# A LayerNorm's shift moved to ScalarE and ahead of other work in a two-layer graph network

## The chip, the cores and the metric

The kernel runs on one core of one Trainium2 chip. Its time is the device time of one execution in microseconds, lower is better; where several executions were measured, the median is given. The profile is of one further execution of the same program.

The core has five engines that run side by side, each with a queue of its own: TensorE (PE, matrix products), VectorE (DVE), ScalarE (ACT), GpSimd (POOL), and SyncE (SP), which here only starts transfers. Each engine takes its instructions in the order in which the program lists them, and an instruction waits at the head of its queue until what it reads is there.

## The reference

There are 128 samples. Each has 128 nodes with 512 features (`x`) and a 128x128 matrix (`adj`) of zeros and ones. Two residual layers follow each other; cut to what matters:

```python
# layer 0: graph attention with 8 heads of 64 features
feats = einsum('bnf,hfu->bhnu', x, W)
dense = e_self[..., :, None] + e_neigh[..., None, :]        # scores of node i and node j
dense = leaky_relu(dense, 0.2) + NEG_BIG * (1 - adj)        # mask
att   = softmax(dense)
x     = layernorm(x + relu(att @ feats + b))                # "first LayerNorm"
# layer 1: two hypergraph convolutions
out = Dn * (H @ (Be * (H.T @ (x @ W)))) + b                 # one convolution; H = (adj != 0)
h = layer_norm(relu(conv1(x)))                              # 512 -> 1024 features
y = conv2(h)                                                # 1024 -> 512, the "second convolution"
x = layernorm(x + (y + x))
```

Everything is float32. The LayerNorms' weights and the biases come in as inputs.

## The kernel before

The kernel handles two samples (a "pair") at a time, 64 pairs. Up to five pairs are in work at once: while one pair's scores are computed, the pair before it is in the attention, the one before that in the convolutions. Every step is registered with a lag (how many rounds after its pair's start) and a time within the round, whose length in this list is 38.6:

```python
T = 38.6
...
time += (p + lag) * T
...
for _, fn, args in sorted(todo, key=lambda e: e[0]):
    fn(*args)
```

The times set nothing but the order in which the instructions stand in the engines' queues. The chip then runs as fast as the waits let it.

The attention scores of a pair lie in `nb` (128 rows, two samples, 8 heads x 128). They arrive by a transfer that spreads a row over all partitions, and pass four engines in four groups `(g, q)` (sample, half of the heads): GpSimd adds the mask, ScalarE adds the node's own score and applies the leaky ReLU, VectorE takes the negated maximum, ScalarE the exponential.

```python
def masked(p, s, g, q):                      # GpSimd, 128x512
    ...
    nc.gpsimd.tensor_tensor(t, t, neg[...], op=ALU.add)

def leaky(p, s, g, q):                       # ScalarE, four of 128x128
    ...
        nc.scalar.activation(t, t, AF.Prelu, bias=s["ft"][:, g, h, 0:1], alpha=SLOPE)

def largest(p, s, g, q):                     # VectorE, "first maximum" is that of group (0, 0)
    ...
    nc.vector.tensor_reduce(s["nm"][:, g, hs], ..., AX.XY, ALU.max, negate=True)

for (g, q), tm, (lag, tl), (lagx, tx), te, tt in (
    ((0, 0), 31.0, (1, 33.2), (1, 33.9), 2.7, 18.1), ((0, 1), 32.2, (1, 35.0), (1, 36.7), 4.6, 18.15),
    ((1, 0), 34.2, (1, 37.5), (2, 2.0), 7.8, 21.5), ((1, 1), 35.4, (2, 6.0), (2, 7.3), 7.9, 21.55),
):
    at(1, tm, masked, g, q)
    at(lag, tl, leaky, g, q)
    at(lagx, tx, largest, g, q)
    at(2, te, exponential, g, q)
    at(2, tt, e_transpose, g, q, since=1)
```

The pair before it is at its first LayerNorm in the same stretch. VectorE adds the residual and takes mean and variance (`mv`), VectorE adds epsilon, GpSimd raises to the power -1/2 (`rs`), GpSimd makes the shift, minus mean times `rs` (`sh`), and ScalarE gives the output:

```python
def residual(p, s, g):
    y = s["y"][:, g, :]
    nc.vector.scalar_tensor_tensor(y, y, 0.0, s["x"][:, g, :], op0=ALU.max, op1=ALU.add)
    moments(p, s, "a", y, g)                 # bn_stats, bn_aggr -> s["mv", "a"]

def rstds(p, s, key):
    ...
    nc.vector.tensor_scalar(ve, s["mv", key][:, :, 1], EPS, None, op0=ALU.add)
    s["rs", key] = small.tile([P, 2], F32, tag="rs", name=f"rs{key}_{p}")
    nc.gpsimd.tensor_tensor(s["rs", key], ve, mhalf, op=ALU.pow)

def first_output(p, s, g):
    t = s["y"][:, g, :]
    nc.scalar.activation(
        t, t, AF.Identity, bias=s["sh"][:, g:g + 1], scale=s["rs", "a"][:, g:g + 1]
    )

at(2, 34.5, first_output, 0)
at(2, 34.55, first_output, 1)
```

The first product of the convolutions reads this output. It is the first matmul of the next round, and ScalarE evicts it (`zT`) for the hidden products `ph`:

```python
at(3, 0.0, propagate, 0)                     # TensorE: pz = y, R
at(3, 0.9, propagate, 1)
at(3, 1.1, z_evict, 0)                       # ScalarE: zT = pz
at(3, 2.0, z_evict, 1)
chain("ph", 3, (2.0, 3.8, 5.6, 7.35, 9.1, 12.65, 14.4, 4.0, 7.5, 11.0), hidden, HALF)
```

The matrix products of a pair are done with seven block products in place of eight. They run into three PSUM banks X, Y and W in the order 1, 2, 6, 5, 7, 4, 3 (the first seven times in the list), with X copied by ScalarE after products 1, 6 and 7 (the last three times). For the second convolution (`py`) that is:

```python
chain("py", 3, (24.2, 29.4, 27.7, 32.9, 31.2, 35.35, 37.1, 26.2, 29.6, 33.1), weigh,
      QU, 1, until=LAST)
...
at(3, 31.3, y_sum, 0, 0, 0, "Y", until=LAST)
at(3, 34.9, y_sum, 1, 1, 2, "W", until=LAST)   # VectorE: third copy + bank W after product 5
at(4, 0.1, y_sum, 0, 1, 1, "W", until=LAST)    # VectorE: second copy + bank W after product 3
at(3, 37.2, y_sum, 1, 0, None, "X", until=LAST)  # ScalarE: bank X after product 4
```

Product 3 adds on to bank W, so it waits until the sum of the second line has read that bank. Between these, VectorE also evicts the propagator (`r_evict`, 35.8, which needs the transferred `dnb`) and works out the deviation of the hidden layer (`h_rstd`, 36.0). The attention's transposes (`e_transpose`, `eT`) follow on VectorE at 18.1 and 21.5, the attention's products (`attend`, `pav`) at 20.65 and 25.95 on TensorE.

Of the kernel before, what the change touches and what calls it, by code (L numbers as in the profile page):

```python
# [8 lines left out]
F32 = mybir.dt.float32  # L9
AF = mybir.ActivationFunctionType  # L10
ALU = mybir.AluOpType
# [9 lines left out]
def kernel(  # L21
# [45 lines left out]
    nc = tc.nc  # L67
    G, N, F = x.shape
    P = 128
# [15 lines left out]
    small = ctx.enter_context(tc.tile_pool(name="small", bufs=4))  # L85
# [212 lines left out]
    LAST = PAIRS - 1  # L298
    steps = []

    def step(lag, time, since=0, until=PAIRS):

        def keep(fn):
            steps.append((lag, time, fn.__name__, range(since, until), fn, ()))
            return fn
        return keep

    def at(lag, time, fn, *args, since=0, until=PAIRS):
        steps.append((lag, time, fn.__name__, range(since, until), fn, args))
# [331 lines left out]
        )  # L641

    for (g, q), tm, (lag, tl), (lagx, tx), te, tt in (
        ((0, 0), 31.0, (1, 33.2), (1, 33.9), 2.7, 18.1), ((0, 1), 32.2, (1, 35.0), (1, 36.7), 4.6, 18.15),
        ((1, 0), 34.2, (1, 37.5), (2, 2.0), 7.8, 21.5), ((1, 1), 35.4, (2, 6.0), (2, 7.3), 7.9, 21.55),
    ):
        at(1, tm, masked, g, q)
# [4 lines that stand above are left out]
# [64 lines left out]

    at(2, 26.2, residual, 0)
    at(2, 30.7, residual, 1)
    at(2, 31.5, rstds, "a")

    @step(2, 33.0)
    def first_shift(p, s):
        s["sh"] = small.tile([P, 2], F32, tag="sh", name=f"sh_{p}")
        for g in range(2):
            nc.gpsimd.tensor_scalar(
                s["sh"][:, g:g + 1], s["mv", "a"][:, g, 0:1], -1.0, s["rs", "a"][:, g:g + 1],
                op0=ALU.mult, op1=ALU.mult,
            )

    def first_output(p, s, g):  # L730
# [2 lines left out]
            t, t, AF.Identity, bias=s["sh"][:, g:g + 1], scale=s["rs", "a"][:, g:g + 1]  # L733
        )

    at(2, 34.5, first_output, 0)
    at(2, 34.55, first_output, 1)

    def skip(p, s, g):

# [116 lines left out]
    def weigh(s, i, to, start):  # L857
# [3 lines left out]
          QU, 1, until=LAST)  # L861
# [10 lines left out]
            nc.vector.tensor_tensor(dst, s["py", i][:, :n], s["py", where][:, :n], op=ALU.add)  # L872

    at(3, 31.3, y_sum, 0, 0, 0, "Y", until=LAST)
    at(3, 34.9, y_sum, 1, 1, 2, "W", until=LAST)
    at(4, 0.1, y_sum, 0, 1, 1, "W", until=LAST)
    at(3, 37.2, y_sum, 1, 0, None, "X", until=LAST)

# [211 lines left out]
    for p in range(PAIRS):  # L1090
        if p > 1:
            todo.append(({2: 79.5, 3: 143.1}.get(p, p * T), load, (p,)))
            todo.append((16.2 if p == 2 else p * T + 19.0, load_blocks, (p,)))
            todo.append((p * T + 28.5, load_edges, (p,)))
        for lag, time, name, pairs, fn, args in steps:
            if p not in pairs:
                continue
            if p == 0 and lag == 2 and time < 8.5:
                time *= 0.2
            if p == LAST:  # L1100

                time = {
                    ("attend", 0): 24.25, ("attended", 0): 25.5, ("add_bias", 0): 25.6,
                    ("attend", 1): 25.95, ("attended", 1): 26.0, ("add_bias", 1): 26.1,
                    ("residual", 1): 26.3, ("rstds", "a"): 26.4, ("first_shift",): 27.0,
                }.get((name,) + args[:1], time)
            if p == LAST - 1:
                time = {
                    ("product", 2): 24.22 if (lag, time) > (3, 20.0) else time,
                    ("squares", 0): 26.5, ("squares", 1): 26.6, ("h_sums", 2): 22.3,  # L1110
                    ("sum_squares",): 43.0, ("h_rstd",): 43.2, ("y_scale", 1): 5.8, ("y_scale", 0): 5.9,
                }.get((name,) + args[:1], time)
            time += (p + lag) * T
            todo.append((
                first.get((name, p) + args, first.get((name, p), time)), run, (fn, p, args)
            ))
# [46 lines left out]
```

## Time and profile before

| | us |
|---|---|
| median of 3 executions | 2557.31 |
| lowest, highest | 2553.69, 2558.03 |
| profiled execution | 2555.38, span of the instructions 2553.3 |

| operation (engine) | mean ns of one | times |
|---|---|---|
| mask (GpSimd, 128x512) | 1277 | 256 |
| power for the first LayerNorm (GpSimd, 128x2) | 700 | 64 |
| shift (GpSimd, 128x1) | 273 | 128 |
| epsilon for the first LayerNorm (VectorE, 128x2) | 418 | 64 |
| first output (ScalarE, 128x512) | 806 | 128 |
| leaky ReLU (ScalarE, 128x128) | 390 | 1020 |
| maximum (VectorE, 128x512) | 681 | 256 |
| sum with bank W (VectorE, 128x256) | 411 | 126 |

How to read the profile: each engine's busy time is given with its share of the span, and "PEld" is TensorE's loading of weights, which overlaps its products. A line of a timeline has the start in us from the span's start, the duration, the engine, the kernel's line, the operation, what it writes and reads, and in square brackets the idle time of the engine before it with what ended that. A line of the waits has who waited for whom, the sum in us, how many times, and the longest. Names are those of the program: `nb` scores, `rsa` the power for the first LayerNorm, `vea` its input, `sh` shift, `y` the first LayerNorm's output, `pz`, `zT`, `phX`, `pyW` as above.

### The profile page before, as it was taken

The page shows a single profiled execution, that of the slowest core. Times are in us where ns is not written, and L with a number is a line of the kernel's source. Part 1 is how long each engine was busy: PE and PEld are TensorE (multiplying, and loading weights), DVE is VectorE, ACT ScalarE, POOL GpSimd, SP SyncE. Part 2 cuts the span into 40 slices and gives each one's busy share as a digit, 9 for nine tenths or more (in the row PEclk, how much of TensorE's full clock was granted, in tenths as well). Part 3 has the DMA queues.
Part 4 walks back from the last instruction along what each step waited for, and adds up shares of the span by engine and source line. Part 5 has one row for each costly group of instructions (what it writes and reads, how often), then busy time and mean ns, then how long its engine had stood idle before and what let it go on. Part 6 is the DMA issues. An engine that isn't in the chain of part 4 may idle for free.

```text
span 2553.3 us, 48482 instructions
## 1 busy us (share of the span) xinstructions
PE 2508.8 (98%) x16349; PEld 2273.2 (89%) x16349; DVE 2120.4 (83%) x4584; ACT 1509.8 (59%) x4289; POOL 1769.9 (69%) x1934
## 2 busy tenths in 40 slices
PE   6999999999999999999999999999999999999998
PEld 5898989999999999999989998999899899889997
DVE  6888888888888888888888888888888888887875
ACT  4565655655655656656556556566565565565662
POOL 5767677676676676676776766766767667767764
PEclk9999999999999999999999999999999999999999
DMA  5444445444444444454444444444444444444430
GB/s 177 130 141 141 133 127 145 131 137 144 135 134 138 141 138 134 141 143 133 127 144 130 136 144 137 134 134 142 139 135 130 143 131 135 141 133 139 134 122 34
DMA packets 420840, 343.75 MB, mean 135 GB/s; under 512 B 141272, under 2 KB 370160, under 8 KB 420592
## 3 DMA queue, kind: packets, MB, share of 16 engines
q1 hardware_dynamic: 417120, 336.19, 44.5%
q10 hardware_dynamic: 3472, 4.47, 0.5%
q8 instruction: 130, 2.13, 0.3%
q14 instruction: 118, 0.97, 0.1%
HBM read 238.83 MB, written 101.71 MB: 133 GB/s over the span
## 4 chain that ended last, share of the span: by engine, by line
PE 83%; DMA 8%; ACT 3%; POOL 2%; DVE 2%; issue 1%; SPq 0%; POOLq 0%; DVEq 0%; ACTq 0%
PE phX L790 18%; PE pyX L473 11%; PE phW L790 9%; PE pfX L473 9%; PE pav L662 7%; PE pyW L473 6%; DMA nb<-rd 4%; PE phY L790 4%; PE pfW L473 4%; PE pq L913 4%; PE pz L755 3%; PE pyY L473 3%; PE pfY L473 2%; ACT nb L592 2%; DMA w<-in_adj_dram 1%
## 5 line engine op out<-in xcount | busy, mean ns | idle before, releaser
L790 PEld LDWEIGHTS phX<-zS,w_sb 128*128 128x128 f32 x3072 | 363.1, 192 | 33.0 <-issue 31.3
L329 ACT COPY py<-pyX 128x257 f32<-128x257 f32 x189 | 70.6, 374 | 538.2 <-PE pyX L473 525.4
L576 POOL TENSOR_TENSOR nb<-nb,neg 128x512 f32<-128x512 f32 x256 | 324.1, 1277 | 79.6 <-DMA nb<-rd 46.6
L790 PE MATMUL phX<-zS,w_sb 128*128 128x128 f32 x3072 | 374.4, 275 | 2.2 <-POOL xS L455 1.3
L841 POOL TENSOR_TENSOR sq<-sq 128x512 f32<-128x512 f32 (+2 forms) x384 | 342.3, 892 | 20.7 <-ACT sq L830 0.6
L592 ACT ACTIVATE nb<-nb,ft 128x128 f32<-128x128 f32 x1020 | 323.9, 390 | 26.6 <-POOL nb L576 25.3
L606 ACT ACTIVATE nb<-nb,nm 128x128 f32<-128x128 f32 x1024 | 320.2, 392 | 0.4 <-DVE nm L598 0.4
L693 DVE SCALAR_TENSOR_TENSOR y<-y,x 128x512 f32<-128x512 f32 x128 | 154.8, 1209 | 151.7 <-POOL y L686 151.7
L709 POOL TENSOR_TENSOR rso<-veo,mhalf 128x2 f32<-128x2 f32 x63 | 44.1, 700 | 332.5 <-DVE veo L707 218.0
L820 ACT ACTIVATE h<-h,vecs 128x128 f32<-128x128 f32 x768 | 244.8, 392 | 34.4 <-DVE h L805 34.4
L662 PEld LDWEIGHTS pav<-ft,eT 128*128 128x128 f32 x2048 | 248.2, 192 | 8.9 <-DVE eT L639 0.8
L598 DVE TENSOR_REDUCE nm<-nb 128x4 f32<-128x512 f32 x256 | 174.3, 681 | 98.3 <-POOL rsa L709 79.9
L473 PE MATMUL pyW<-w_sb,hS 128*128 128x256 f32 x1008 | 240.7, 381 | 4.1 <-DVE y L872 4.1
L473 PE MATMUL pyX<-w_sb,hS 128*128 128x257 f32 x1008 | 242.6, 382 | 0.6 <-ACT py L329 0.6
L662 PE MATMUL pav<-ft,eT 128*128 128x65 f32 x2048 | 242.6, 272 | 0.1
L473 PE MATMUL pyX<-w_sb,h 128*128 128x257 f32 x1008 | 239.4, 379 | 0.0
L473 PEld LDWEIGHTS pyW<-w_sb,hS 128*128 128x128 f32 x1008 | 191.3, 190 | 33.5 <-DVE y L872 6.1
L473 PEld LDWEIGHTS pyX<-w_sb,hS 128*128 128x128 f32 x1008 | 186.1, 190 | 25.1 <-POOL y L686 0.9
L473 PEld LDWEIGHTS pyX<-w_sb,h 128*128 128x128 f32 x1008 | 186.4, 190 | 24.7
L686 POOL TENSOR_TENSOR y<-y,b_bc 128x512 f32<-128x512 f32 x128 | 162.4, 1269 | 62.5 <-DVE y L677 62.4
L455 POOL TENSOR_TENSOR xS<-xT 128x256 f32<-128x256 f32 x124 | 117.8, 950 | 106.8 <-DVE xT L370 89.4
L329 ACT COPY ph<-phX 128x512 f32<-128x512 f32 x192 | 112.3, 585 | 101.5 <-PE phX L790 98.7
(166 smaller groups left out, 5887.3 us busy)
## 6 DMA issues: line engine op xcount, KB each, us to landing
nb<-rd SPq DMA_DIRECT2D x127, 512.0 KB, 6.2
ed<-nb SPq DMA_DIRECT2D x126, 512.0 KB, 3.1
eb<-ed SPq DMA_DIRECT2D x504, 128.0 KB, 2.9
x<-in_x_dram SPq DMA_DIRECT2D x64, 512.0 KB, 7.1
out_dram<-o SPq DMA_DIRECT2D x63, 512.0 KB, 2.8
xb<-in_x_dram SPq DMA_DIRECT2D x248, 128.0 KB, 2.9
a<-in_adj_dram SPq DMA_DIRECT2D x64, 128.0 KB, 6.3
w<-in_adj_dram SPq DMA_DIRECT2D x128, 64.0 KB, 4.4
```

Source lines behind the costliest of these rows:

```text
L329: nc.scalar.copy(t[:, :n], s[kind, "X"][:, :n])
L473: nc.tensor.matmul(to[:, :n], lhs[:, k, :], rhs[:, k, :n], start=bool(start) and k == 0, stop=(k == nk - 1), skip_group_check=True,)
L576: nc.gpsimd.tensor_tensor(t, t, neg[:, :, None, :].to_broadcast([P, NB, HH, B]), op=ALU.add)
L592: nc.scalar.activation(t, t, AF.Prelu, bias=s["ft"][:, g, h, 0:1], alpha=SLOPE)
L598: nc.vector.tensor_reduce(s["nm"][:, g, hs], scores(p, s, g, hs).rearrange("p b h j -> p h b j"), AX.XY, ALU.max, negate=True,)
L606: nc.scalar.activation(t, t, AF.Exp, bias=s["nm"][:, g, h:h + 1])
L662: nc.tensor.matmul(t[:, h * (U + 1):(h + 1) * (U + 1)], s["eT"][:, g, q * HH + h, :], s["ft"][:, g, q * HH + h, 2:], start=True, stop=True,)
L686: nc.gpsimd.tensor_tensor(s["y"][:, g, :], s["y"][:, g, :], b0_bc, op=ALU.add)
L693: nc.vector.scalar_tensor_tensor(y, y, 0.0, s["x"][:, g, :], op0=ALU.max, op1=ALU.add)
L790: nc.tensor.matmul(to[:, m * N:(m + 1) * N], w[:, k, m * P:(m + 1) * P], rhs[:, k, :], start=bool(start) and m == 0 and k == 0, stop=(k == ...
L820: nc.scalar.activation(dst[:, k, :], src[:, k, :], AF.Relu, bias=b1_sb[:, c:c + 1])
L841: nc.gpsimd.tensor_tensor(t[:, :n, :], t[:, :n, :], t[:, n:2 * n, :], op=ALU.add)
```

## The change

Three things are moved. The epsilon and the power of the first LayerNorm stand ahead of the four masks of the next pair, where before the power stood after the first mask. The shift is no longer made by GpSimd but by ScalarE, in three small activations (negated mean of both samples, then its product with `rs` for each), and the first output follows it at once, ahead of the first leaky ReLUs. The sum that frees bank W stands ahead of the first maximum on VectorE, which itself moves behind the deviation of the hidden layer.

The purpose is that the first product of the next round does not depend on the masks, nor on the transfer for which they wait, and that product 3 does not depend on the first maximum.

For the last pair the shift had a time of its own, which falls away; in the pair before it, product 5 of the second convolution comes ahead of product 7.

```diff
-        ((0, 0), 31.0, (1, 33.2), (1, 33.9), 2.7, 18.1), ...
+        ((0, 0), 31.0, (1, 33.2), (1, 36.1), 2.7, 18.1), ...
@@
     at(2, 30.7, residual, 1)
-    at(2, 31.5, rstds, "a")
-
-    @step(2, 33.0)
+    at(2, 30.8, rstds, "a")
+
+    @step(2, 33.12)
     def first_shift(p, s):
         s["sh"] = small.tile([P, 2], F32, tag="sh", name=f"sh_{p}")
+        nm = small.tile([P, 2], F32, tag="nmean", name=f"nmean_{p}")
+        nc.scalar.activation(nm, s["mv", "a"][:, :, 0], AF.Identity, scale=-1.0)
         for g in range(2):
-            nc.gpsimd.tensor_scalar(
-                s["sh"][:, g:g + 1], s["mv", "a"][:, g, 0:1], -1.0, s["rs", "a"][:, g:g + 1],
-                op0=ALU.mult, op1=ALU.mult,
+            nc.scalar.activation(
+                s["sh"][:, g:g + 1], nm[:, g:g + 1], AF.Identity,
+                scale=s["rs", "a"][:, g:g + 1],
             )
@@
-    at(2, 34.5, first_output, 0)
-    at(2, 34.55, first_output, 1)
+    at(2, 33.13, first_output, 0)
+    at(2, 33.14, first_output, 1)
@@
-    at(3, 34.9, y_sum, 1, 1, 2, "W", until=LAST)
+    at(3, 33.9, y_sum, 1, 1, 2, "W", until=LAST)
@@ (the last pair)
-                    ("residual", 1): 26.3, ("rstds", "a"): 26.4, ("first_shift",): 27.0,
+                    ("residual", 1): 26.3, ("rstds", "a"): 26.4,
@@ (the pair before it)
                     ("product", 2): 24.22 if (lag, time) > (3, 20.0) else time,
+                    ("product", 5): 29.5 if (lag, time) > (3, 20.0) else time,
```

More of the change, by code (lines that the diff above doesn't have):

```diff
@@ L643 @@
     for (g, q), tm, (lag, tl), (lagx, tx), te, tt in (
-        ((0, 0), 31.0, (1, 33.2), (1, 33.9), 2.7, 18.1), ((0, 1), 32.2, (1, 35.0), (1, 36.7), 4.6, 18.15),
+        ((0, 0), 31.0, (1, 33.2), (1, 36.1), 2.7, 18.1), ((0, 1), 32.2, (1, 35.0), (1, 36.7), 4.6, 18.15),
         ((1, 0), 34.2, (1, 37.5), (2, 2.0), 7.8, 21.5), ((1, 1), 35.4, (2, 6.0), (2, 7.3), 7.9, 21.55),
```

## The prediction

> **What bounds the kernel now.** I read the page first (busy times), then TensorE's waits, then the timeline of one middle round on four engines, then the timelines of the first and last rounds, and at last the distances of these events in the 61 rounds of the middle. A round is one pair of samples; I mark its start by the first matmul of `pz` (line 755).
>
> ```profile
> span 2553.3 us, 48482 instructions
> ...
> PE 2508.8 (98%) x16349; PEld 2273.2 (89%) x16349; DVE 2120.4 (83%) x4584; ACT 1509.8 (59%) x4289; POOL 1769.9 (69%) x1934
> ```
>
> The reader is to see that TensorE is busy for all but 44.5 us of the span. Nothing here can gain more than some 2% unless it shortens a matmul, and the change touches none. So the question is only which of the few waits of TensorE it removes or makes.
>
> ```profile
> PE pz L755 <- ACT y L732: 12.9, 2, 9.5
> PE phX L790 <- ACT zT L767: 8.7, 18, 0.7
> ...
> PE pyW L473 <- DVE y L872: 4.1, 3, 3.4
> ```
>
> These rows (line that waited, line waited for: total us, times, longest) are the ones that the change can reach. They count only what TensorE was seen idle. The distance from one `pz` to the next shows more: it is 38.66 or 38.67 us in the undisturbed rounds, and the 61 rounds from 100.53 to 2475.20 us take 2374.67 us, so 2374.67 - 61 x 38.665 = 16.1 us are lost. Going through the starts of the matmuls in these rounds, 12.1 us of it lie between `pz` and the first `ph` product (about 20 rounds, 0.1 to 0.9 us each), 1.2 us before the last `py` product. One such round (columns: start, duration, engine, line, operation, count; in brackets the idle time before it and what ended it):
>
> ```profile
> 1305.74 1.95 PE L755 MATMUL pz<-R,y 128*128 128x128 f32 x16
> 1307.94 2.05 PE L790 MATMUL phX<-zT,w_sb 128*128 128x128 f32 x16 [0.25 <-ACT zT L767]
> ```
>
> ```profile
> 1301.01 1.28 ACT L592 ACTIVATE nb<-nb,ft 128x128 f32<-128x128 f32 x4 [0.49 <-POOL nb L576]
> 1303.30 1.52 ACT L732 ACTIVATE y<-y,sh,rsa 128x512 f32<-128x512 f32 x2 [1.02 <-POOL sh L725]
> 1304.73 1.26 ACT L592 ACTIVATE nb<-nb,ft 128x128 f32<-128x128 f32 x4
> ...
> 1306.15 1.27 ACT L592 ACTIVATE nb<-nb,ft 128x128 f32<-128x128 f32 x4
> 1307.33 1.04 ACT L767 COPY zT<-pz 128x512 f32<-128x512 f32 x2
> ```
>
> ```profile
> 1299.70 1.27 POOL L576 TENSOR_TENSOR nb<-nb,neg 128x512 f32<-128x512 f32 x1 [1.31 <-issue]
> 1301.08 0.70 POOL L709 TENSOR_TENSOR rsa<-vea,mhalf 128x2 f32<-128x2 f32 x1
> 1301.74 1.28 POOL L576 TENSOR_TENSOR nb<-nb,neg 128x512 f32<-128x512 f32 x1
> 1303.00 0.51 POOL L725 TENSOR_SCALAR sh<-mva,rsa 128x1 f32<-128x1 f32 x2
> 1303.46 2.51 POOL L576 TENSOR_TENSOR nb<-nb,neg 128x512 f32<-128x512 f32 x2
> ```
>
> The reader is to follow one chain backwards. `ph` starts at 1307.94, when ScalarE has evicted `zT` (from 1307.33). ScalarE would have done so at 1.09 us after `pz` began, as in the undisturbed rounds, but the third group of leaky ReLUs stood before it. That queue began late: ScalarE finished the first leaky group and then sat idle for 1.02 us until GpSimd gave the shift at 1303.00, because GpSimd had the mask of 1299.70, the power `rsa`, and a second mask ahead of it. The mask of 1299.70 was itself late: GpSimd waited 1.31 us, with no releaser named here ("issue"); in about every second round the same wait is put down to the transfer of `nb`, so I take it for that. In the 61 rounds the first mask starts 5.6 to 7.3 us before `pz`; where it is later than about 6.4 us before, the `zT` eviction comes late.
>
> The two ends of the program are larger. In the last round but one:
>
> ```profile
> 2504.36 0.70 POOL L709 TENSOR_TENSOR rsa<-vea,mhalf 128x2 f32<-128x2 f32 x1 [3.30 <-DVE vea L707]
> 2505.02 5.17 POOL L841 TENSOR_TENSOR sq<-sq 128x512 f32<-128x512 f32 x6
> 2510.17 0.50 POOL L725 TENSOR_SCALAR sh<-mva,rsa 128x1 f32<-128x1 f32 x2
> ```
>
> ```profile
> 2511.34 3.78 PE L755 MATMUL pz<-R,y 128*128 128x128 f32 x16 [3.40 <-ACT y L732]
> ```
>
> The power was ready at 2505.06, but the shift stood behind six additions of squares (5.17 us). TensorE waited 3.40 us, and then ran slowly: `pz` and the first `ph` product, 1.79 us each in a normal round, spread from 2511.34 to 2517.71. In the first round TensorE likewise waits 9.49 us and starts `pz` at 52.97, where the power was ready at 48.33, two masks and two shifts earlier.
>
> **What the Trainium skill says.** PSUM — Partial Sum Buffer, section Engine vs sequencer instructions: the queues of ScalarE, VectorE and GpSimd are strictly first in, first out. The trace agrees: the shift stood 5.17 us behind squares it doesn't need. ScalarE: Activation LUTs, section What ACT_TABLE_LOAD costs: an activation costs 186 ns plus 0.833 ns an element, and some 93 ns for each pointer operand; neighbours overlap by 93 ns. The first output (512 elements, two pointers) would be 799 ns; it took 806. TensorE: Matmul & The Clock Gate, section Part 1: after an idle window of about 3.4 us the array falls to half its clock. `pz` after the wait of 3.40 us took 3.78 us where 1.95 us is usual, which agrees. SBUF — State Buffer, section Who interferes with whom: a VectorE `tensor_scalar` in a two-port mode and a GpSimd operation exclude each other. The deviation's addition on VectorE agrees: its mean is 0.42 us, the same operation in the last LayerNorm takes 0.17 us, and in the round shown it ended as the mask ended.
>
> **The change, part by part.**
>
> Deviation ahead of the masks. On VectorE the addition now follows the moments directly; on GpSimd the power comes before the first mask. The moments end 5.75 us before `pz` in nearly all rounds. Add 0.04 to the next instruction, 0.17 for the addition with no mask in its way, 0.08 to GpSimd and 0.70 for the power (row `rsa`): the power ends 4.76 us before `pz`, as it did before (4.7). The four masks follow at 1.25 us each: they end 3.5, 2.25, 1.0 before and 0.25 after `pz`, where a good round had the third at 1.7 before. The masks lose about 0.7 us, and the wait for `nb` disappears: its rows arrive 5.6 us before `pz` at the latest, and the masks now start at 4.7.
>
> Shift and output on ScalarE. Two GpSimd operations of 0.26 us go. Three small activations come; the negated mean needs only the moments, so it hides ahead of the power. The two shifts take an estimated 0.4 to 0.55 us by the ScalarE page's figures (two starts 187 to 280 ns apart), so the first output starts 4.3 to 4.15 us before `pz`, where it was 3.05 in good rounds and 2.0 to 2.5 in disturbed ones. From there ScalarE runs on: two outputs 1.43, three leaky groups 1.17 each, one copy 0.25, starts counted to starts, sum 5.2. So `zT` can be evicted 0.9 to 1.05 us after `pz`; 1.09 is free. All three masks are in time for their groups (2.75, 1.6 and 0.15 us before `pz`). So the 12.1 us go, by a narrow margin.
>
> Sum of the second convolution ahead of the first maximum. The sum can run when product 5 has ended, 4.1 us before `pz`; before, it stood behind a maximum that waited for the first leaky group. The 1.2 us before the last `py` product go. The maximum moves behind the deviation of the hidden layer, whose propagator eviction waits for a transfer in 37 rounds. So VectorE is later by up to one maximum, 0.6 us, early in the round. From the eviction's lateness to the transposes of the attention there is slack: evictions 2.9 or 1.6 us before `pz` both gave a first transpose ending 19.92 after it. Attention needs it at 20.51. I allow 2 us for the ten or so rounds with an eviction later than that.
>
> First rounds. `pz` of pair 0 no longer waits for two masks and a dilated shift: output at 48.75 in place of 52.10, 3.35 us. In the next round TensorE waited 3.40 us for the moved sum, which stood behind a first maximum and the node degrees of a later pair (ends at 96.65 in place of about 93.5). That wait goes, but there the moments come late, and ScalarE's chain of 5.2 us from a first output at about 93.9 brings `zT` to 99.1, `ph` to 99.7 in place of about 102.3: 2.6 us.
>
> Last rounds. Output follows the power at once, at 2505.4 in place of 2510.47. `pz` then starts when the last `py` product ends, 2507.8. Wait 3.4, slow clock in `pz` about 1.8 and in `ph` 1.0, the rest of the eviction's delay 0.2: 6.4 us. Product 5 ahead of product 7 in the last pair but one removes the 0.56 us wait of product 7 for its copy, but product 4 then waits as long for the next copy: 0.
>
> Sum: 12.1 + 1.2 + 3.35 + 2.6 + 6.4 = 25.7 gained, 2 lost to the attention, and 3 kept back for the narrow margin. 20.7 us, so 2557.3 - 20.7 = 2536.6, rounded to 2537.
>
> **Rivals.** First, ScalarE becomes the bound at the head of the round. If the small activations take 0.3 us more than I reckon, `zT` is late in every round and not in a third: 61 x 0.2 = 12 us eat the steady gain; the time would be about 2547 to 2550. For it speaks the margin of 0.04 to 0.2 us; against it, that ScalarE stands idle for 0.5 us before the power ends. Second, VectorE's later maximum pushes the transposes beyond 20.51 in most rounds: 0.2 to 0.4 us a round, 12 to 24 us, and the time stays at 2540 to 2560. For it speaks that VectorE is busy nearly without a gap from the eviction to the transposes; against it, the slack of about a us just named. Third, the gains at the ends are given back: with `pz` earlier, the first products meet other waits (weights, transposes of the next pair), so 6 us are lost and 2543 remain.
>
> **Range and chances.** The three measured times of before lie 4.3 us apart, and the profiled one (2555.4) in the middle. With no rival I expect 2532 to 2537, with one of the first two 2545 to 2557. I take 2527 to 2552. Two per cent faster would be 2506, more than all idle time of TensorE together; two per cent slower would need 0.8 us lost in every round beside the lost gains.
>
> **What would show it.** Right: no TensorE wait for the first output and almost none for `zT`; GpSimd waiting for the addition before `rsa` in each round and not for `nb`; no 3.4 us wait at the last `pz`; rounds of 38.67. Wrong: `zT` waits in most rounds (first rival), `pav` waiting for `eT` (second), new waits of `ph` for `zS` or `xS` in the first round (third).

## The result, and the profile after

The changed kernel takes 2572.5 us (median; 2571.8 to 2574.0), the kernel before, run beside it, 2557.7 us: a ratio of 1.006, 95% interval 1.0043 to 1.0078. It is slower by some 15 us, where 20 us less were predicted. The profiled execution grew from 2553.3 to 2570.0 us.

The page of the changed kernel, its first two rows:

```profile
span 2570.0 us, 48486 instructions
...
PE 2530.1 (98%) x16349; PEld 2266.9 (88%) x16349; DVE 2114.2 (82%) x4584; ACT 1535.0 (60%) x4481; POOL 1753.4 (68%) x1806
```

TensorE is as full as before, 98%. Its 16349 matmuls are the same, yet its busy time grew by 21.3 us, more than the span: so the page counts short waits between matmuls as busy time, and the loss has to be read from the starts. TensorE's waits of the changed kernel (who waited for whom: total us, times, longest):

```profile
PE phW L792 <- DVE h L807: 6.7, 11, 0.7
PE pz L757 <- ACT y L734: 6.0, 1, 6.0
PE phX L792 <- ACT zT L769: 2.5, 1, 2.5
```

The wait of `phX` for `zT`, 18 times before, is left once, at the second round. The wait of `pz` for the output is left in the first round, 6.0 us in place of 9.5. The wait of `pyW` for VectorE's sum is gone. But a new row has come, `phW` for the hidden layer's sum on VectorE. As before, this view shows only a part of the loss, so I take the starts of `pz` again. Three stretches add up to the whole: up to the third `pz`, 139.20 us before and 135.68 now, 3.5 us gained; from there 60 rounds, 2336.0 us before and 2362.6 now, 26.6 us lost; and from the last but one `pz` to the end 78.1 us before and 71.7 now, 6.4 us gained. Together 16.7 us lost, 0.44 us in each round of the middle.

What the change wanted in a round, it got. ScalarE and GpSimd in a middle round whose `pz` starts at 1239.17 (timelines of the changed kernel):

```profile
1234.68 0.48 ACT L727 ACTIVATE sh<-nmean,rsa 128x1 f32<-128x1 f32 x2 [0.64 <-POOL rsa L709]
1235.07 1.51 ACT L734 ACTIVATE y<-y,sh,rsa 128x512 f32<-128x512 f32 x2
1236.48 2.44 ACT L592 ACTIVATE nb<-nb,ft 128x128 f32<-128x128 f32 x8
...
1239.07 1.28 ACT L592 ACTIVATE nb<-nb,ft 128x128 f32<-128x128 f32 x4
1240.26 0.58 ACT L769 COPY zT<-pz 128x512 f32<-128x512 f32 x1
```

```profile
1233.94 0.70 POOL L709 TENSOR_TENSOR rsa<-vea,mhalf 128x2 f32<-128x2 f32 x1 [1.95 <-DVE vea L707]
1234.61 4.96 POOL L576 TENSOR_TENSOR nb<-nb,neg 128x512 f32<-128x512 f32 x4
...
1241.82 0.78 POOL L780 TENSOR_TENSOR zS<-zT 128x256 f32<-128x256 f32 x1 [0.86 <-ACT zT L769]
```

The shifts start when the power ends, the output 0.39 us later, and ScalarE works on without a gap until it evicts `zT` at 1240.26, which is 1.09 us after `pz`. The four masks run as one block and, but for one round of the middle, no longer wait for a transfer. VectorE, first in a round of the kernel before (its `pz` starts at 490.13), where the first maximum stands behind an idle time of 1.38 us:

```profile
486.26 0.69 DVE L598 TENSOR_REDUCE nm<-nb 128x4 f32<-128x512 f32 x1 [1.38 <-POOL rsa L709]
486.86 0.41 DVE L872 TENSOR_TENSOR y<-py,pyW 128x256 f32<-128x256 f32 x1
```

and now in the changed kernel:

```profile
1235.31 0.42 DVE L874 TENSOR_TENSOR y<-py,pyW 128x256 f32<-128x256 f32 x1 [1.11 <-PE pyW L473]
1236.91 0.42 DVE L437 TENSOR_TENSOR R<-pd,dnb 128x256 f32<-128x256 f32 x1 [1.18 <-DMA dnb<-dd_d]
1237.25 1.11 DVE L891 TENSOR_TENSOR m<-y 128x1 f32<-128x1 f32 x1
...
1238.80 0.80 DVE L896 SCALAR_TENSOR_TENSOR veh<-veh,m 128x2 f32<-128x2 f32 x1
...
1239.73 1.28 DVE L598 TENSOR_REDUCE nm<-nb 128x4 f32<-128x512 f32 x2
...
1241.26 1.88 DVE L905 SCALAR_TENSOR_TENSOR y<-y,rsh,bw_bc 128x512 f32<-128x512 f32 x2
```

Here is what the prediction missed. The deviation of the hidden layer (`m`, `veh`) isn't done until 1239.80. `m` takes 1.11 us where it takes 0.15 when nothing stands in its way, and the operation at 1238.80 takes 0.80 where it takes 0.16. The first ends at 1238.36, the second at 1239.60; the third mask ends about 1238.35 and the fourth at 1239.57. Only then come two maxima (before, the first of them had been done in an idle moment), and then the scaling (two operations at L905, the second convolution's sum times the hidden deviation's inverse), which is stretched to 1.88 us. From there to the attention's transposes VectorE is idle for only 0.6 us in all and about 1 us late, and this is where it reaches TensorE. VectorE, ScalarE and TensorE later in that round:

```profile
1252.79 0.64 DVE L807 TENSOR_TENSOR h<-ph,phW 128x512 f32<-128x512 f32 x1
```

```profile
1253.47 1.28 ACT L822 ACTIVATE h<-h,vecs 128x128 f32<-128x128 f32 x4 [1.58 <-DVE h L807]
...
1256.85 0.36 ACT L329 COPY pf<-pfX 128x264 f32<-128x264 f32 x1
```

```profile
1256.27 1.05 PE L473 MATMUL pfY<-w_sb,xT 128*128 128x264 f32 x4
1257.35 1.13 PE L473 MATMUL pfX<-w_sb,xS 128*128 128x264 f32 x4
...
1260.38 1.97 PE L662 MATMUL pav<-ft,eT 128*128 128x65 f32 x16
```

ScalarE waits 1.58 us for the hidden sum, so it comes late to the copy that `pf` needs: the third `pf` product starts 1.08 us after the second, where 0.89 is usual. `pav` starts late because the attention's transpose ended late. Added up over the rounds from the second `pz` on, against the spacing of undisturbed rounds, the late starts are 9.6 us at the last `phW` product, 15.2 us at the `pf` products and 17.7 us at `pav` and the product behind it: 42.5 us, against the some 13 us of waits that the change removed there.

Medians over the middle rounds, in us from `pz`, with two of the experiments below. The edges are the step on VectorE behind the scaling and the maximum that follows it, and the row of the transposes gives their start:

| | before | changed | degrees late | fourth mask late |
|---|---|---|---|---|
| propagator evicted from | -2.03 | -2.09 | -2.30 | -2.09 |
| hidden deviation ends | 0.52 | 0.63 | -0.24 | -0.23 |
| VectorE begins the edges | 3.41 | 4.49 | 3.14 | 3.66 |
| sum for the last `phW` | 12.64 | 13.60 | 11.59 | 12.91 |
| first attention transpose begins | 19.39 | 20.35 | 18.70 | 19.65 |
| first `pav` product | 20.51 | 21.19 | 20.51 | 20.51 |
| mean round | 38.93 | 39.38 | 38.68 | 38.86 |

### The profile page after: what moved, and what is told of

It reads as the page before. It is cut to its first block, busy times and chain, and to the rows that moved or that the text cites. A ratio compares the mean times of both kernels' runs of the same rounds, so it can differ in the third digit from the quotient of the medians.

```text
span 2570.0 us, 48486 instructions
## 1 busy us (share of the span) xinstructions
PE 2530.1 (98%) x16349; PEld 2266.9 (88%) x16349; DVE 2114.2 (82%) x4584; ACT 1535.0 (60%) x4481; POOL 1753.4 (68%) x1806
## 4 chain that ended last, share of the span: by engine, by line
PE 83%; DVE 7%; DMA 4%; issue 2%; ACT 2%; POOL 1%; SPq 1%; DVEq 0%; POOLq 0%; ACTq 0%
PE phX L792 14%; PE pyX L473 14%; PE pfX L473 9%; PE phW L792 8%; PE pav L662 8%; PE pyW L473 7%; PE pfW L473 4%; PE pz L757 4%; PE phY L792 4%; PE pq L915 3%; PE pyY L473 3%; PE pfY L473 2%; DMA dnb<-dd_d 2%; ACT nb L592 1%; DVE o L745 1%
## 5 line engine op out<-in xcount | busy, mean ns | idle before, releaser
L576 POOL TENSOR_TENSOR nb<-nb,neg 128x512 f32<-128x512 f32 x256 | 317.8, 1273 | 14.3 <-DMA nb<-rd 14.3
L592 ACT ACTIVATE nb<-nb,ft 128x128 f32<-128x128 f32 x1020 | 317.3, 389 | 7.1 <-POOL nb L576 7.1
L598 DVE TENSOR_REDUCE nm<-nb 128x4 f32<-128x512 f32 x256 | 168.0, 676 | 2.9 <-ACT nb L592 2.2
L627 DVE STREAM_TRANSPOSE eT<-eb 128x512 f32<-128x512 f32 x252 | 161.9, 678 | 0.0
```

The source lines that it names most:

```text
L576: nc.gpsimd.tensor_tensor(t, t, neg[:, :, None, :].to_broadcast([P, NB, HH, B]), op=ALU.add)
L598: nc.vector.tensor_reduce(s["nm"][:, g, hs], scores(p, s, g, hs).rearrange("p b h j -> p h b j"), AX.XY, ALU.max, negate=True,)
L627: nc.vector.transpose(s["eT"][:, g, hs, :].rearrange("p h (b i) -> p h b i", b=NB), s["eb", g][:, :, hs, :].rearrange("p b h j -> p h b j"),)
```

## The experiments

Theory: VectorE had no room in the stretch from `pz` to the attention; the first maximum, taken out of an idle moment and put there, makes it late, and TensorE waits. Rivals: the block of masks alone is to blame, ScalarE's three new activations are, or the LayerNorm's part itself.

| kernel | us | ratio to before, 95% interval |
|---|---|---|
| sum and maximum moved only | 2588.8 | 1.0119, 1.0104 to 1.0134 |
| LayerNorm's part only | 2597.3 | 1.0152, 1.0136 to 1.0167 |
| changed, maximum ahead of the propagator | 2579.9 | 1.0083, 1.0066 to 1.0100 |
| changed, degrees late | 2530.3 | 0.9892, 0.9877 to 0.9906 |
| before, degrees late | 2556.1 | 0.9984, 0.9975 to 0.9992 |
| sum and maximum moved, degrees late | 2555.4 | 0.9986, 0.9977 to 0.9994 |
| ends only | 2549.5 | 0.9966, 0.9957 to 0.9975 |
| before, one maximum twice | 2588.9 | 1.0122, 1.0107 to 1.0137 |
| changed, degrees late, one maximum twice | 2536.8 | 0.9919, 0.9903 to 0.9936 |
| changed, fourth mask late | 2544.1 | 0.9941, 0.9924 to 0.9957 |

**The sum and the maximum alone.** The kernel before with

```diff
-        ((0, 0), 31.0, (1, 33.2), (1, 33.9), 2.7, 18.1), ...
+        ((0, 0), 31.0, (1, 33.2), (1, 36.1), 2.7, 18.1), ...
-    at(3, 34.9, y_sum, 1, 1, 2, "W", until=LAST)
+    at(3, 33.9, y_sum, 1, 1, 2, "W", until=LAST)
```

> Only the sum and the first maximum on VectorE are moved; the first LayerNorm, the last pair and the rest are as before. Theory (VectorE is made late): the maximum leaves a stretch in which VectorE was idle and is paid after the hidden layer's deviation, 0.6 us a round; the waits for zT of before stay (12 us in all), attention and the third product into bank W of ph wait in most rounds. I expect 2560 to 2575 us. Rival (the masks, now in one block of 5 us on GpSimd, hold VectorE back, and not the maximum's place): about 2554 us, 3 us less than before, since only the wait of 3.4 us at the second round goes.

It took 2588.8 us, more than the theory's 2575. The sum for the last `phW` comes 13.67 us after `pz` (12.64 before), as late as in the changed kernel, though masks, power and shift are as before. So the new order on VectorE does harm without the block of masks, and the rival falls. That in this order it is the maximum that costs, and not the sum, is only argued here; what a maximum costs behind `pz` is measured further below. The expectation was too low because the lateness comes round: the moments of the first LayerNorm end 5.51 us before `pz` in place of 5.75, and the late starts behind `pz` grew from 12 to 19 us.

**The LayerNorm's part alone.** The changed kernel with both lines above undone.

> The LayerNorm's part alone (deviation ahead of the masks, shift and output on ScalarE), with the sum and the first maximum where they were before. Theory: the first leaky group now ends only 1.5 us before pz, the maximum waits for it at the head of VectorE's queue, and the sum that frees bank W behind it comes about 0.9 us before pz, when product 3 should have started 1.7 before: TensorE waits about 1 us a round for the sum, and VectorE is later by 1 us or more. I expect 2610 to 2680 us. Rival (the LayerNorm's part is good by itself and the moved maximum does the harm): 2535 to 2545 us.

2597.3 us, 13 us under the expected range: the direction is the theory's, the rival falls. TensorE's waits have one row that matters:

```profile
PE pyW L473 <- DVE y L874: 53.2, 62, 6.3
```

The maximum waits for the first leaky group, which now stands behind the output; the sum waits behind the maximum, and product 3 for the sum, in 62 rounds. So neither half of the change gains anything alone, and the LayerNorm's part needs the sum moved. The expected lateness of VectorE did not come: its deviation ends 0.68 us before `pz`, and with the maximum back in its place the late starts at `phW`, `pf` and `pav` are gone. TensorE's own wait also gives VectorE time here, so this alone does not show that the maximum is to blame.

**The maximum ahead of the propagator.** The changed kernel with the maximum at 35.0 in place of 36.1.

> The changed kernel with the first maximum put between the moved sum and the propagator's eviction, a place where VectorE waits for a transfer. Theory (one maximum of 0.6 us in the wrong place makes VectorE late): most of the waits of attention and bank W go, rounds of 38.67 to 38.9, 2540 to 2555 us. Rival (the block of masks holds the deviation back until 0.4 us after pz, whatever comes before it): the deviation ends where it did, one maximum comes off behind it, 0.6 us less a round as well, but the dilated scaling stays; 2550 to 2560. If the eviction is pushed later than the masks' end, no gain: 2572.

2579.9 us, a miss: I had named no gain at 2572 as the worst case. The maximum stands at the head of the queue until the first leaky group is there, 1.34 us before `pz`; the propagator's eviction moves from 2.09 to 0.73 before `pz` and the deviation ends at 1.23. With the output first, the leaky group comes too late for a place ahead of the eviction. A place between the eviction and the deviation, where VectorE then waits for masks anyway, was not tried.

**The degrees late.** The changed kernel with work that has nothing to do with the change, the node degrees (some 1.25 us on VectorE, and the transfer that carries them on), moved out of the busy stretch into the idle time ahead of the sum:

```diff
-    @step(0, 11.0)
+    @step(0, 33.0)
     def nodes(p, s):
-    @step(0, 17.0)
+    @step(0, 33.5)
     def write_nodes(p, s):
```

> The changed kernel with the node degrees (1.25 us on VectorE) moved out of the stretch between the deviation and the attention's transposes, into the idle time ahead of the moved sum. Theory (VectorE's lateness of about 1 us between pz and the attention is the whole of the loss): all waits of pav, of pf for its copies and of ph for bank W go; rounds of 38.67; 2528 to 2536 us. Rival (the waits of pf come from ScalarE, which got three activations more): pf still waits 0.3 us a round, 2545 to 2555.

2530.3 us, within the theory's range; 42 us less than the changed kernel and 1.1% less than the kernel before. The page and TensorE's waits of this kernel (all rows of 1 us and more):

```profile
span 2528.5 us, 48425 instructions
```

```profile
PE px L382 <- DMA x<-in_x_dram: 8.8, 1, 8.8
PE pz L757 <- ACT y L734: 6.0, 1, 6.0
PE phX L792 <- ACT zT L769: 2.5, 1, 2.5
PE phX L792 <- POOL xS L455: 1.3, 1, 1.3
```

All four are in the first rounds. The rounds of the middle are 38.67 us nearly without exception. The waits of `pf` went too, with the same three activations on ScalarE, so that rival falls. The room helps in a roundabout way as well. VectorE begins the edges 1.35 us earlier, although the degrees had stood behind them: as it is no longer late, the moments of the first LayerNorm end 6.38 us before `pz` in place of 5.50, the block of masks starts 0.88 us earlier, and the hidden deviation ends 0.87 us earlier.

**The degrees late in the other kernels.** The same two lines in the kernel before, and in the one with the sum and the maximum moved only.

> The kernel before with the degrees alone moved late. Theory: VectorE costs the kernel before nothing by itself (TensorE hardly waits for it), the waits for zT come from the masks' transfer and stay, and the two ends stay: 2550 to 2559 us, at most 5 us gained. Rival (the degrees' move is the whole gain of the run with the degrees late): 2530 to 2540 us.

> The run with the degrees late, but with the first LayerNorm as before (power behind the first mask, shift on GpSimd, output behind the first leaky group): what the LayerNorm's part is worth when VectorE has room. Theory: it is worth the waits for zT (12 us) and the two ends (about 10 us), so this kernel takes 2548 to 2556 us. Rival (the gain of the run with the degrees late came from VectorE alone, the LayerNorm's part adds only the ends): 2538 to 2544 us.

2556.1 and 2555.4 us: both as the theory had it. In the kernel before, room on VectorE is worth 0.16%, because there TensorE waits for `zT` and not for VectorE. With the sum and maximum moved it takes away the 31 us that they had cost. Set side by side, the LayerNorm's part is worth 2588.8 - 2572.5 = 16 us where VectorE is late, and 2555.4 - 2530.3 = 25 us where it has room: the prediction's gain was there, and was covered by the loss on VectorE.

**The ends only.** The LayerNorm's part for pairs 0, 1 and the last, the moved sum for pair 0 and product 5 for the last but one; the middle as before. Cut to what matters, against the changed kernel:

```diff
+    at(2, 30.8, rstds, "a", until=2)
+    at(2, 31.5, rstds, "a", since=2)
...
+    for since, until in ((0, 2), (LAST, PAIRS)):
+        at(2, 33.12, first_shift_ends, since=since, until=until)
+        at(2, 33.13, first_output, 0, since=since, until=until)
+        at(2, 33.14, first_output, 1, since=since, until=until)
+    at(3, 33.6, y_sum, 1, 1, 2, "W", until=1)
```

> The change only where the program begins and ends: LayerNorm's part for pairs 0, 1 and the last, the moved sum for pair 0, product 5 for the last pair but one; all the middle as before. Theory (the ends gain 3.5 and 6.4 us in the changed kernel, the middle loses 27): 2546 to 2550 us. Rival (the gain at the ends needs the middle's order): 2555 to 2558 us.

2549.5 us, as expected: about 9 us of gain do not need the middle.

**One maximum twice.** The room on VectorE, measured by itself: the maximum behind the scaling is done twice with the same result, in the kernel before and in the one with the degrees late.

```diff
-        nc.vector.tensor_reduce(
+        for _ in range(2 if (g, q) == (1, 0) and p > 1 else 1):
+            nc.vector.tensor_reduce(
```

> The kernel before, with nothing moved, but the maximum behind the scaling of the second convolution done twice: 0.6 us more on VectorE in each round, at the place where the changed kernel is late. Theory (VectorE has next to no slack there, 0.1 to 0.3 us): 0.3 to 0.6 us a round are lost, 2575 to 2595 us. Rival (about a microsecond of slack, as the prediction had it): no change, 2555 to 2561 us.

> The same doubled maximum in the kernel with the degrees late. Theory (moving the degrees made about 1 us of slack there): no wait comes back, 2530 to 2534 us. Rival (the degrees' move helps in another way than by room on VectorE): 2545 to 2565 us.

2588.9 us: in the kernel before, 0.6 us of work at this place costs 39.46 - 38.93 = 0.53 us a round. Nothing is reordered there, so it is the plain price of the lack of room. With the degrees late the same work costs 0.09 us a round (2536.8 us); that is 3 us above my range, since in some rounds the sum is again just late and the second round has slow products that the run with the degrees late did not have, but far below the rival's.

**The fourth mask late.** The changed kernel with the fourth mask behind the power of the hidden layer:

```diff
-        ... ((1, 1), 35.4, (2, 6.0), (2, 7.3), 7.9, 21.55),
+        ... ((1, 1), 36.05, (2, 6.0), (2, 7.3), 7.9, 21.55),
```

> The changed kernel with the fourth mask put behind the power of the hidden layer on GpSimd, so that the block of masks ends about 0.85 us before pz in place of 0.4 after it. Theory (the block of masks shares a way into the memory with VectorE's two-input operations and holds the hidden layer's deviation until it ends): the deviation ends 0.3 to 0.8 us earlier, around pz, VectorE is in time more often, 2545 to 2563 us, less the dilation of the scaling by the fourth mask. Rival (the deviation waits for the propagator's transfer only): it ends at 0.6 after pz as before, 2570 to 2575 us.

2544.1 us, 28 us less than the changed kernel. The propagator is evicted as before (2.09 us before `pz`), yet the deviation ends 0.23 before `pz` in place of 0.63 after. VectorE and GpSimd of this kernel in a middle round:

```profile
1337.51 0.79 DVE L896 SCALAR_TENSOR_TENSOR veh<-veh,m 128x2 f32<-128x2 f32 x1
```

```profile
1334.55 3.73 POOL L576 TENSOR_TENSOR nb<-nb,neg 128x512 f32<-128x512 f32 x3
1338.58 0.70 POOL L901 TENSOR_TENSOR rsh<-veh,mhalf 128x2 f32<-128x2 f32 x1 [0.30 <-DVE veh L899]
```

The two-input operation on VectorE ends at 1338.30, the block of now three masks at 1338.28. So the deviation was held by the masks and not by the propagator's transfer, and a single mask in another place gives back 28 of the 42 us that moving the degrees gives. The hold itself is not new: in the kernel before, the deviation ended 0.52 us after `pz`. It is why there was no room; what the change added is the maximum and the longer scaling.

## Why the prediction was wrong

- *Right:* ends of the program, last rounds: 6.4 us predicted, 6.4 measured, with `pz` starting as the last `py` product ends. Product 5 ahead of product 7 gave next to nothing, as reckoned: the wait of 0.56 us of product 7 went, and product 4 now waits 0.46.
- *Right in kind, too large:* first rounds, 5.95 us predicted, 3.5 measured. `pz` of pair 0 came 2.9 us earlier in place of 3.35. In the next round `zT` bounds TensorE, as I had reckoned, and it waited 2.51 us, but I left out that it then runs slowly (TensorE of the changed kernel):

```profile
97.11 2.79 PE L792 MATMUL phX<-zT,w_sb 128*128 128x128 f32 x16 [2.51 <-ACT zT L769]
99.69 2.88 PE L792 MATMUL phY<-zT,w_sb 128*128 128x128 f32 x16
```

  These two groups take 2.79 and 2.88 us in place of 1.95, and their starts lose 1.7 us.
- *Right:* ScalarE's chain, with less margin than reckoned. First output 4.10 us before `pz` (predicted 4.3 to 4.15), `zT` at 1.09 without a gap before it (predicted 0.9 to 1.05, and 1.09 free). The 12.1 us went, and the 1.2 us before the last `py` product.
- *Wrong, and it decided:* "From the eviction's lateness to the transposes of the attention there is slack [...] I allow 2 us". In its place the runs showed 42.5 us of late starts. I had read the slack from rounds in which the eviction was late by 1.3 us and the transposes were not. But between the two stands the hidden deviation, and in both kinds of rounds it was held back until the last mask ended. In 59 of the 60 middle rounds of the kernel before it ended 0.75 to 0.82 us after the fourth mask, while the eviction moved between 3.04 and 1.20 us before `pz`. VectorE of the kernel before in a round with an early eviction (`pz` at 800.30, fourth mask done at 800.02) and in one with a late eviction (`pz` at 490.13, fourth mask done at 489.85):

```profile
797.37 0.42 DVE L437 TENSOR_TENSOR R<-pd,dnb 128x256 f32<-128x256 f32 x1
797.70 1.11 DVE L889 TENSOR_TENSOR m<-y 128x1 f32<-128x1 f32 x1
798.74 1.30 DVE L889 TENSOR_TENSOR m<-py 128x1 f32<-128x1 f32 x1
```

```profile
488.63 0.42 DVE L437 TENSOR_TENSOR R<-pd,dnb 128x256 f32<-128x256 f32 x1 [1.36 <-PE pyX L473]
488.97 0.90 DVE L889 TENSOR_TENSOR m<-y 128x1 f32<-128x1 f32 x1
489.79 0.15 DVE L889 TENSOR_TENSOR m<-py 128x1 f32<-128x1 f32 x1
```

  The early eviction only made the two `m` slower, 1.11 and 1.30 us in place of 0.90 and 0.15. The lateness was swallowed there, ahead of the place where the maximum was put. Behind it there was next to no room: one maximum more costs 0.53 us a round. The prediction's own figures already left little: from 19.92 to 20.51 are 0.59 us, no more than one maximum, and in these two rounds the first transpose ended at 20.03 and 20.08, which leaves 0.43 to 0.48.
- *Wrong in size:* "VectorE is later by up to one maximum, 0.6 us". It is 1.08 us later at the edges: 0.6 for the maximum, some 0.1 for the deviation, and 0.36 because the two scalings, which now start 0.72 us later, take a median of 1.88 us in place of 1.52. The traces show where this comes from: the second scaling is longer where it starts after GpSimd's first `zS` operation has begun, 2.65 us after `pz` in most rounds. In the changed kernel it took 1.22 or 1.23 us in the 41 rounds where it did and at most 0.75 in the 19 where it did not; with the sum and the maximum moved and the degrees late, 1.22 to 1.25 us in 29 rounds and at most 0.75 us in 31. No run moved `zS` by itself.
- The second rival came true as far as it went: 17.7 us at `pav`, where it named 12 to 24. It named the attention alone; the 24.8 us at the last `phW` and at `pf` no rival named. The range of 2527 to 2552 didn't even hold the 2560 of its own text.

## What to carry to other kernels

An operation moved out of an engine's idle moment can cost nearly its full time where it lands, even if the sum of the engine's work is unchanged: here 0.53 of 0.6 us where the engine had no room, and 0.09 where it had some. Read slack only behind the point at which the delay will be put in, or measure it: do one operation there twice. And when a change frees one engine and fails, look for unrelated work on the engine that became late that can go into the idle moment: here that turned 0.6% of loss into 1.1% of gain.

## What the runs showed of the hardware

- A small two-input operation on VectorE waits for the GpSimd operation under way: 128x2 elements took 0.80 us in place of 0.16. In the changed kernel 51 of these 63 operations took longer than 0.2 us, and all 51 ended 0.015 to 0.023 us after the end of a GpSimd operation. The Trainium skill has this lock for VectorE operations with two inputs in SBUF (SBUF — State Buffer, section Who interferes with whom); what I had not expected is that a block of masks can hold up a chain of small operations one by one, each until the end of a mask: in the round shown `m` took 1.11 us until the third mask ended, and the 128x2 operation 0.80 until the fourth.
- TensorE ran slowly after an idle time of 2.51 us (2.79 us in place of 1.95), at a granted clock of 0.72 from 97.10 to 99.70 us and 0.65 from there to 102.50. The wait is shorter than the idle window of about 3.4 us of the Trainium skill's page TensorE: Matmul & The Clock Gate, section Part 1. But the wait's length does not decide it: with the degrees late the same wait of 2.51 us was followed by groups of 2.05 and 1.95 us at a granted clock of 1.00.
